# Preparing gate and up inside the attentions, and four pairs of blocks by two levels in the first pass

## The chip, the cores and the metric

The kernel runs on one core of a Trainium2 chip. The metric is device time in microseconds (us) of one execution. Its engines are TensorE (PE; its weight loads are shown as PEld), VectorE (DVE), ScalarE (ACT), GpSimd (POOL) and SyncE (SP), which here only issues transfers. Each engine works through its own instructions in order and waits on semaphores for the others.

## The reference

One decoder layer in float32 on x of 16 batches x 128 rows x 1024 columns, with a context of the same shape:

```python
x = x + self_attention(layernorm(x))            # one head, width 256; Wqkv, Wo
x = x + linear_cross_attention(layernorm(x), ctx)  # 8 heads x 64
x = x + ffn(layernorm(x))
# ffn: 4-bit weights, w = (nibble - zero) * scale per group of 64
Wg, Wu, Wd = dequantize(gate), dequantize(up), dequantize(down)
h = silu(x @ Wg.T) * (x @ Wu.T)                 # 1024 -> 2752
out = h @ Wd.T                                  # 2752 -> 1024
```

The cross attention takes the softmax of the queries over the 64 channels of a head and of the keys over the positions, forms the 64 x 64 context of each head, multiplies, projects, and normalises each column.

## The kernel before, in words

**The feed-forward products are done by Strassen's scheme in Winograd's form**: seven products of half-size blocks in place of eight. The inter dimension of 2752 is cut into ten blocks of 256 (numbers 0 to 9) and a remainder (RB = 10). The tokens are taken in two passes: batches 8 to 15 first (pass 0), then 0 to 7 (pass 1), since the cross attention works on 8 to 15 first.

*By one level* (`one_block`, L1178): gate and up of one block are 7 products each, in the order GATE. A product (`products`, L1140) is four matmuls of 128 x 128 weights with 512 columns, each of which the trace shows as two instructions. The operands T are half-blocks of the normalised x; the weights of all seven products, sums included, lie ready in DRAM (`wprep`).

*By two levels* (`two_levels`, L1360): a pair of blocks (gate and up of both) is seven outer products in the order DOWN, each of them again seven inner ones: 49 products of four matmuls with 256 columns. The left inner operands `li` are combined by POOL (`inner_left`, L1338), the right ones `ti` by DVE (`Operands.inner_right`), four for each outer product. DVE also adds the banks into U, V and C (`got`), and after outer products 2, 3, 7 and 4 ACT takes Silu and DVE multiplies gate with up into `h` (`finish`). In the program the order around outer product n is, on PE: 6, 2, 5, 4 of n, 1 of n+1, 3 of n, 7 of n+1; the `ti` of n+1 are made while n runs. At the end of each outer product the function `between` is called.

Pass 0 does blocks 0 to 5 by one level, pair 3 (blocks 6 and 7) by two, blocks 8 and 9 by one, and then the remainder (`last_block`). Pass 1 does all five pairs by two levels and keeps most right operands from pair to pair. In pass 0 nothing is kept.

**Preparation** (`prepare`, L205) turns the packed bytes into `wprep`. It is a generator that is advanced step by step between other work. A job is one matrix (g, u or d for down) of one block: two steps of dequantising (two shifts or masks of 128 x 512 integers, a subtraction and a multiplication of 128 x 1024, all on DVE, tiles `pa`) and a step of four combinations (`pc`). A job loads two `raw` tiles and their scales and zeros, and stores seven tiles of 256 KB. The remainder has its own jobs r (one step) and m. There are 33 jobs: 20 of g and u, r, m, and 11 of d. Before the change `early` does the first ten (blocks 0 to 4, EARLY = 5) within the self attention, with stores through POOL's queue, and `rest` does the other 23 in pass 0, d and the others in turn, through SP's queue; `beside` and `between` say after which product a step is taken.

**Order.** DVE, PE and SP instructions of the cross attention and of most of what follows are held in program order (`InOrder`). Instructions without that wrapper are placed by the framework's scheduler by the time at which it reckons them ready; on each engine they then run in that order. PE's instructions of block 0 are free in this sense, so that they fill the end of the cross attention.

**The cross attention** works in ticks (`later`, `tick`): eight per batch, one after each key unit and each query unit. The functions of a query unit are put off by ticks: `weigh` (row sums on DVE, multiplication on POOL, tile `qe`), `turn` (DVE transposes into `kt`, SP stores `kd`), `load` one tick later (SP loads `qs`, which must wait until `kd` has landed). `project_out` multiplies `qs` with the mixed context `m_sb` some ticks later and adds the result to X.

**Memory** is given out as stacks from both ends of the SBUF. A later pool lies where an earlier one was, and its first tiles wait until the old ones were last read. On the left, over the self attention's `a_g`, `a_w` (weights `wqkv_sb`, `wo_sb`, biases), come the cross attention's `b_cx` (8 KB per partition), `b_w` (4), `b_0` (8), `b_ek` (12), `b_as` (4), `b_3` in this order, and over these the feed-forward's `c_w` (weights, 20 KB), `c_t`, `c_h`. `block_loads` brings the x of a pass back from DRAM, in eight loads.

Of the kernel before, what the change touches and what calls it, by code (L numbers as in the profile page):

```python
# [66 lines left out]
def decoder_layer(  # L67
# [95 lines left out]
    def prep_pools(stack, name, c, ahead):  # L163
        for key, bufs in (("a", 3), ("c", c), ("raw", ahead + 1), ("sz", ahead + 1)):
            pools[key] = stack.enter_context(
                tc.tile_pool(name=f"{name}_{key}", bufs=bufs, side="right", reuse_waits="tile")
            )
# [4 lines left out]
    def load_raw(blk, mat, s):  # L172
# [3 lines left out]
        if mat == "d":  # L176
            raw, sz = raw[:w], pools["sz"].tile([P, 2, 512], F32, name="szd")[:w]
            nc.sync.dma_start(raw, dq[ds(start // 2, w), ts(s, 512)])
            for g in range(w // 32):
                row = dsz[start // GROUP + g, ts(s, 1024)].rearrange("(t f) -> t f", t=2)  # L180
                nc.sync.dma_start(sz[ts(g, 32)], row.partition_broadcast(32))
# [13 lines left out]
        for m, off, w in parts:  # L195
            q, szs = matrices[m]
            nc.sync.dma_start(raw[:, :, ds(at, w)], q[:, :, ds(off, w)])
            nc.sync.dma_start(
# [6 lines left out]
    def prepare(jobs, ahead, queue, vector=nc.vector):  # L205
# [3 lines left out]
        loads = deque(load_raw(*u) for u in units[:ahead])  # L209
# [6 lines left out]
        for k, (blk, mat, s) in enumerate(units):  # L216
# [6 lines left out]
            if k + ahead < len(units):  # L223
                loads.append(load_raw(*units[k + ahead]))
# [61 lines left out]
    EARLY = 5  # L286

    def give_half(b, h, oT, wo_d, psum, tensor=nc.tensor, vector=nc.vector):
# [19 lines left out]
    prep_pools(first, "q", 4, 1)  # L308
    early = prepare(
        [(blk, mat) for blk in range(EARLY) for mat in "gu"], 1, nc.gpsimd, InOrder(tc, nc.vector)  # L310
    )
    give_pool = ExitStack()
    ag = give_pool.enter_context(tc.tile_pool(name="a_g", bufs=1, reuse_waits="tile"))
    with (
# [166 lines left out]
        for t in range(NT):  # L481
# [38 lines left out]
            else:  # L520

                for i in range(1, BPT):
                    give((t - 1) * BPT + i - 1, oT)
                    value(i, xnT, v)
                atT = turn_weights(at)
# [76 lines left out]
    bcx = unit_pool("b_cx", 2)  # L602
    bw = unit_pool("b_w", 1)
    b0 = unit_pool("b_0", 2)
    bek = unit_pool("b_ek", 3)
    bas = unit_pool("b_as", 1)
    b3 = unit_pool("b_3", 3)
    bkt = side_pool("b_kt", 3)
# [3 lines left out]
    bqs = side_pool("b_qs", 5)  # L612
    b1 = side_pool("b_1", 1)
    b2 = side_pool("b_2", 2)
    bps = side_pool("b_ps", 3, space=PSUM)

# [15 lines left out]
    if True:  # L632
# [8 lines left out]
        sync.dma_start(wk_sb, xwk)  # L641
        sync.dma_start(wq_sb, xwq)
        sync.dma_start(wv_sb, xwv.rearrange("(r p) s -> p r s", p=P))
        sync.dma_start(xwo_sb, xwo.rearrange("(r p) o -> p r o", p=P))
        sync.dma_start(xbo_sb, xbo)
        sync.dma_start(gs_sb, xg)
# [43 lines left out]
        def load_ctx(b):  # L690
# [236 lines left out]
        for d in range(2):  # L927
            wo_again.append(bqs.tile([P, C], F32, name="wo_again", tag="qs"))
            sync.dma_start(wo_again[d], wo[ts(d, P)])
# [12 lines left out]
        for k, b in enumerate(batches):  # L942
# [13 lines left out]
            if len(ahead) == 2:  # L956
                later(2, lambda n=ahead[1]: ctxs.update({n: load_ctx(n)}))
# [68 lines left out]
    with ExitStack() as gs:  # L1026
# [9 lines left out]
        def attention_done():  # L1036

            nonlocal rest
            if plain:
                raise_flag()  # L1040
            sides.close()
            prep_pools(second, "f", 4, 2)
# [858 lines left out]
```

## Time and profile before

| | |
|---|---|
| runs | 2240.55, 2241.54, 2241.73 us; median 2241.54 |
| profiled execution | 2241.3 us; its span 2239.5 us |
| busy in the span | PE 2204.4, DVE 1482.2, POOL 553.1, ACT 468.9 us |
| self attention | 0 to about 250 us |
| cross attention, a batch every 31.2 us | 250 to about 757 us |
| blocks 0 to 5 by one level (block 0 beside the attention's end) | 762 to 1074 us |
| pair 3 by two levels | 1074 to 1162 us |
| blocks 8 and 9, remainder | 1162 to 1299 us |
| pass 1: five pairs, remainder | 1299 to 1760 us |
| down projection | 1760 us to the end |

In the lines below, a group of instructions has its line, engine, operation, output<-input, shapes and count, then the busy time and the mean of one in ns, then the engine's idle time in front of them and who ended it. A line of waits has the total, how often, and the longest. A line of windows has the stretch, its length, and then the busy time of PE, PEld, DVE, ACT and POOL (each with its count), the clock that PE was granted, the share of the 16 DMA engines that was busy, and GB/s.

### The profile page before, as it was taken

Reading aid. Unit: us, or ns where it says so; the run is one execution under the profiler, and the core shown is the slowest. Engines: PE = TensorE matmul, PEld = TensorE weight load, DVE = VectorE, ACT = ScalarE, POOL = GpSimd, SP = SyncE. Lnnn points to the kernel's source line nnn. Section 1 sums busy time; section 2 is a strip of 40 time slices with the busy share of each in tenths; the row PEclk is TensorE's granted clock in tenths of the full one; section 3 lists DMA queues with packets and bytes.
Section 4 is the critical chain, followed back from the end, with each engine's and each line's share of the span. In section 5 each row is a group of like instructions: output and inputs, shape, how many; then the busy total and the mean of one; then the engine's idle time right before and its main releaser. Section 6 shows DMA issues by size and latency. Waiting matters only on the chain.

```text
span 2239.5 us, 24114 instructions
## 1 busy us (share of the span) xinstructions
PE 2204.4 (98%) x8330; PEld 1517.3 (68%) x8330; DVE 1482.2 (66%) x2055; ACT 468.9 (21%) x651; POOL 553.1 (25%) x543
## 2 busy tenths in 40 slices
PE   8999899999999999999999999999999999999998
PEld 7556555555555544444774488888887688888887
DVE  6997466667667657666796658787787645544462
ACT  2111135454554431111111112121121000000000
POOL 5452044444444400001320044444442000000000
PEclk9999999999999999999999999999999999999999
DMA  6435246666686768887649834454554964333731
GB/s 251 157 130 169 85 132 198 209 205 197 208 258 192 225 182 287 284 267 253 199 166 301 251 100 158 167 197 155 175 198 165 350 211 164 114 125 129 226 118 39
DMA packets 270835, 425.23 MB, mean 190 GB/s; under 512 B 28784, under 2 KB 130544, under 8 KB 270576
## 3 DMA queue, kind: packets, MB, share of 16 engines
q1 hardware_dynamic: 244624, 377.72, 52.5%
q0 software_dynamic: 8064, 27.27, 3.3%
q10 hardware_dynamic: 18016, 18.62, 2.7%
q8 instruction: 68, 1.11, 0.2%
q14 instruction: 63, 0.52, 0.1%
HBM read 265.62 MB, written 157.35 MB: 189 GB/s over the span
## 4 chain that ended last, share of the span: by engine, by line
PE 90%; DVE 6%; issue 2%; DMA 1%; POOL 1%; ACT 0%; SPq 0%; DVEq 0%; POOLq 0%; ACTq 0%
PE po L1780 21%; PE q L63 20%; PE p L63 18%; PE kq L63 9%; PE mm L63 8%; PE kx L63 5%; PE mm L396 4%; PE mm L411 2%; DVE pa L63 2%; PE p L1157 1%; PE mm L292 1%; PE tr L343 1%; DVE ti L63 1%; DMA wo_again<-in_wo 0%; POOL qe L806 0%
## 5 line engine op out<-in xcount | busy, mean ns | idle before, releaser
L63 PE MATMUL p<-b,w 128*128 128x512 f32 x560 | 248.2, 596 | 1.9 <-DVE sg L63 1.9
L63 PE MATMUL q<-ti,li 128*128 128x256 f32 x1008 | 232.2, 379 | 3.5 <-DVE ti L63 2.8
L63 POOL TENSOR_TENSOR li<-w 128x512 f32<-128x512 f32 x84 | 118.1, 1408 | 433.3 <-DMA w<-wu 244.8
L63 PEld LDWEIGHTS q<-ti,li 128*128 128x128 f32 x1008 | 191.0, 190 | 31.3 <-issue 2.8
L63 PEld LDWEIGHTS p<-b,w 128*128 128x128 f32 x560 | 106.9, 191 | 136.4 <-issue 128.8
L1780 PE MATMUL po<-wc,lc 128*128 128x256 f32 x840 | 183.4, 379 | 0.0
L63 PE MATMUL p<-T,w 128*128 128x512 f32 x400 | 177.2, 592 | 0.0
L1780 PEld LDWEIGHTS po<-wc,lc 128*128 128x128 f32 x840 | 159.6, 190 | 21.8
L63 ACT COPY k<-q 128x512 f32<-128x512 f32 x126 | 73.7, 585 | 399.2 <-PE q L63 399.2
L63 PEld LDWEIGHTS p<-T,w 128*128 128x128 f32 x400 | 76.0, 190 | 95.7 <-issue 95.2
L1780 PE MATMUL po<-wq,lq 128*128 128x256 f32 x560 | 126.7, 379 | 0.2 <-issue 0.2
L806 POOL TENSOR_TENSOR qe<-qe,qrec 128x1024 f32<-128x1024 f32 x64 | 122.0, 1906 | 11.5 <-DVE qrec L63 9.3
L63 PEld LDWEIGHTS mm<-qs,m_sb 128*128 128x128 f32 x512 | 97.3, 190 | 40.1 <-issue 26.8
L63 PE MATMUL kq<-wk_sb,cx 128*128 128x512 f32 x256 | 120.4, 592 | 2.5 <-DMA cx<-in_cx 2.5
L63 PE MATMUL kx<-ek,cxt 128*128 128x512 f32 x256 | 121.8, 598 | 0.0
L63 PE MATMUL mm<-qs,m_sb 128*128 128x256 f32 x512 | 120.8, 379 | 0.0
L63 PE MATMUL kq<-wq_sb,xn 128*128 128x512 f32 x256 | 120.3, 593 | 0.0
L1780 PEld LDWEIGHTS po<-wq,lq 128*128 128x128 f32 x560 | 106.0, 190 | 15.8 <-issue 0.8
L63 DVE TENSOR_TENSOR pa<-pa,sz 128x1024 f32<-128x1024 int32 x86 | 112.6, 1309 | 2.5
L396 PE MATMUL mm<-xnT,wqkv_sb 128*128 128x512 f32 (+1 forms) x320 | 112.9, 509 | 0.0
L63 DVE STREAM_TRANSPOSE kt<-qe 128x1024 f32<-128x1024 f32 x64 | 79.5, 1242 | 43.7 <-POOL qe L806 43.5
L727 ACT ACTIVATE ek<-kq 128x1024 f32<-128x1024 f32 x64 | 65.3, 1020 | 147.4 <-PE kq L63 147.4
(201 smaller groups left out, 3595.7 us busy)
## 6 DMA issues: line engine op xcount, KB each, us to landing
w<-wu SPq DMA_DIRECT2D x140, 256.0 KB, 3.6
lq<-h SPq DMA_DIRECT2D x140, 256.0 KB, 4.4
w<-wg SPq DMA_DIRECT2D x138, 256.0 KB, 2.8
kd<-kt SPq DMA_DIRECT2D x64, 512.0 KB, 2.9
qs<-kd SPq DMA_DIRECT2D x256, 128.0 KB, 3.2
h<-hc SPq DMA_DIRECT2D x80, 256.0 KB, 2.8
wq<-wd SPq DMA_DIRECT2D x70, 256.0 KB, 5.3
h<-h SPq DMA_DIRECT2D x60, 256.0 KB, 3.0
```

Of the source, the lines that this page charges most:

```text
L63: return lambda *args, **kw: self._tc.keep_in_program_order(fn(*args, **kw))
L292: tensor.matmul(ps, oT[:, d, ts(b % BPT, S)], wo_d[d][:, ts(h, 512)], start=(d == 0), stop=(d == 1),)
L343: nc.tensor.transpose(tr[:, j, :], xn[:, ts(4 * h + j, P)], ident)
L396: nc.tensor.matmul(ps[:, tokens], wqkv_sb[:, f, c, :], xnT[:, c, tokens], start=(c == 0), stop=(c == CC - 1),)
L411: nc.tensor.matmul(ps, xnT[:, c, ts(i, S)], wqkv_sb[:, 4:6, c, :], start=(c == 0), stop=(c == CC - 1),)
L727: nc.scalar.activation(ek, ps, AF.Exp)
L806: nc.gpsimd.tensor_tensor(qe, qe, rec.unsqueeze(2).to_broadcast(wide), ALU.mult)
L1157: tensor.matmul(ps, wt[:, j, :], T[q][:, :, j], start=(first == q and j == 0), stop=(q in (2, 3, 4) and j == JC - 1), skip_group_check=True,)
L1780: nc.tensor.matmul(bank[:, i, :], l[:, ts(i, S)], w,  start=(start and c == 0 and i % 2 == 0), stop=(stop and c == len(pairs) - 1), skip_g ...
```

## The change

- The 33 jobs stand in one list, `todo`: all g and u, then r and m, then the d. `early` takes the first 11 (to g of block 5), with three more steps in the self attention's last quarter. A new generator `middle` takes the next 12 (the rest of g and u, r, m, and d of block 0) within the cross attention, two steps per batch and three in every third, 35 calls; its loads and stores go through SP's queue in program order. `rest` has the ten d that remain, in pass 0.
- Pass 0 does blocks 0 and 1 by one level and the pairs 1 to 4 by two. `rest` is advanced after outer products 1, 2, 6 and 5 of a pair (before: 1, 6 and 5).
- The pools of `middle` (28 KB) come to the right side; `kt` goes from 3 to 2 buffers, `qs` from 5 to 4. On the left the order is now `b_ek`, `b_as`, `b_cx`, `b_0`, `b_w`, `b_3`.
- The cross attention's first loads (its weights, the first two contexts, `wo_again`) are no longer held in program order.
- The first four weight tiles of the feed-forward are loaded through POOL's queue (before: the first through POOL's, the others through SP's).
- The x of pass 1 is loaded in one go after the pairs; before, its eight loads were spread over blocks 8 and 9 and the remainder. The outer operands that need it move from the remainder's start to its m products.

```diff
-    def prep_pools(stack, name, c, ahead):
-        for key, bufs in (("a", 3), ("c", c), ("raw", ahead + 1), ("sz", ahead + 1)):
+    def prep_pools(stack, name, a, ahead):
+        for key, bufs in (("a", a), ("c", 4), ("raw", ahead + 1), ("sz", ahead + 1)):
...
+    todo = [(blk, mat) for blk in range(RB) for mat in "gu"] + [(RB, "r"), (RB, "m")]
+    todo += [(blk, "d") for blk in range(len(BLOCKS))]
+    EARLY, MIDDLE = 11, 23
...
-    prep_pools(first, "q", 4, 1)
-    early = prepare(
-        [(blk, mat) for blk in range(EARLY) for mat in "gu"], 1, nc.gpsimd, InOrder(tc, nc.vector)
-    )
+    prep_pools(first, "q", 3, 1)
+    early = prepare(todo[:EARLY], 1, nc.gpsimd, InOrder(tc, nc.vector))
...
                     give((t - 1) * BPT + i - 1, oT)
                     value(i, xnT, v)
+                    next(early, None)
...
-    bcx = unit_pool("b_cx", 2)
-    bw = unit_pool("b_w", 1)
-    b0 = unit_pool("b_0", 2)
     bek = unit_pool("b_ek", 3)
     bas = unit_pool("b_as", 1)
+    bcx = unit_pool("b_cx", 2)
+    b0 = unit_pool("b_0", 2)
+    bw = unit_pool("b_w", 1)
     b3 = unit_pool("b_3", 3)
-    bkt = side_pool("b_kt", 3)
+    bkt = side_pool("b_kt", 2)
...
-    bqs = side_pool("b_qs", 5)
+    bqs = side_pool("b_qs", 4)
...
+    prep_pools(sides, "x", 2, 1)
+    middle = prepare(todo[EARLY:MIDDLE], 1, sync, vector, sync)
...
-            sync.dma_start(wo_again[d], wo[ts(d, P)])
+            nc.sync.dma_start(wo_again[d], wo[ts(d, P)])
...
+            for n in (3, 5, 7) if k % 3 == 0 and ahead else (3, 7) if ahead else ():
+                later(n, lambda: next(middle, None))
...
-            rest = prepare(jobs, 2, nc.sync, vector)
+            rest = prepare(todo[MIDDLE:], 2, nc.sync, vector)
...
-        PAIRS = [3]
+        PAIRS = [1, 2, 3, 4]
...
-            load_weights(nc.gpsimd if n == 0 else nc.sync)
+            load_weights(nc.gpsimd)
...
                 elif blk == RB:
-                    steps = n in (0, 2, 4)
+                    steps = n in (0, 1, 2)
                 else:
-                    steps = (1, 1 + (mat == "g" and blk < 3), 1, 0, 1, 0, 0)[n % 7]
+                    steps = (1, 1 + (mat == "g"), 1, 0, 1, 0, 0)[n % 7]
...
-            if pass1 and n % 3 == 0:
-                next(pass1_loads, None)
...
-                for k in {("r", 0): (5,), ("r", 1): (7,), ("m", 6): (6,)}.get((mat, q), ()):
+                for k in {("m", 7): (5,), ("m", 6): (7,), ("m", 2): (6,)}.get((mat, q), ()):
                     outer_operand(T1, k)
...
-                    0, PAIRS, first_operands, lambda q: q in (1, 6, 5) and next(rest, None)
+                    0, PAIRS, first_operands, lambda q: q in (1, 2, 6, 5) and next(rest, None)
...
-                pass1_loads = block_loads(1, pass1)
+                for _ in block_loads(1, pass1):
+                    pass
```

## The prediction

> **What bounds the kernel now.** First the page's engine rows, then the list of what TensorE (PE) waited for, then single stages, since the shares are averages.
>
> ```profile
> PE 2204.4 (98%) x8330; PEld 1517.3 (68%) x8330; DVE 1482.2 (66%) x2055; ACT 468.9 (21%) x651; POOL 553.1 (25%) x543
> ```
>
> PE is busy for 2204.4 of 2239.5 us, so 35 us are idle. The largest waits:
>
> ```profile
> PE tr L343 <- ACT xn L152: 9.4, 1, 9.4
> PE p L1157 <- DMA w<-wg: 4.9, 1, 4.9
> PE q L63 <- DVE ti L63: 3.3, 4, 2.4
> PE mm L63 <- DMA wo_again<-in_wo: 3.1, 1, 3.1
> PE kq L63 <- DMA cx<-in_cx: 2.5, 1, 2.5
> ```
>
> So only fewer PE instructions can bring much, and whatever serves PE must keep up. The table of stages shows how far DVE is from that: one batch of the cross attention, four and a half one-level blocks, and the one pair by two levels in the first pass (from its first DVE sum to its last).
>
> ```profile
> 531.23:562.46 31.23, 31.23 (x109) 17.78 (x108) 21.78 (x28) 15.92 (x20) 13.68 (x16) 1.00 0.65 197
> 853.00:1074.00 221.00, 221.00 (x511) 97.73 (x512) 148.32 (x203) 27.22 (x46) 6.25 (x4) 0.99 0.82 267
> 1081.65:1166.30 84.65, 81.32 (x367) 69.09 (x366) 76.07 (x93) 15.04 (x23) 32.64 (x22) 1.00 0.49 160
> ```
>
> After the span and PE's busy time come PEld, DVE, ACT, POOL, clock, DMA share. In the pair DVE is busy for 76.1 of 84.7 us; this is the only stage of the first pass where PE waits for DVE repeatedly (the 3.3 us above). There POOL also stretches DVE's work:
>
> ```profile
> L63 DVE TENSOR_TENSOR pa<-pa,sz 128x1024 f32<-128x1024 f32 x3 | 6.5, 2174 | 0.1
> L63 DVE TENSOR_TENSOR pa<-pa,sz 128x1024 f32<-128x1024 int32 x3 | 4.6, 1540 | 0.1
> L63 DVE TENSOR_SCALAR pa<-raw 128x512 int32<-128x512 int32 x6 | 3.4, 602 | 0.0
> ```
>
> Three dequantisings cost 14.5 us here, 4.83 each; the same four instructions away from POOL's combinations take 0.76 + 2.48 = 3.24 us (DVE's timeline at 190 us).
>
> **1. PE work removed.** PE's timeline gives 3.435 us per product of a one-level block (8 instructions of 512 columns) and 1.727 us per product of a pair (8 of 256 columns). A block is 14 products, 48.1 us; two blocks 96.2. A pair is 49 products, 84.6 us. Three more pairs remove 3 x 11.6 = 34.8 us of PE time. That is the most the change can take from PE's own list.
>
> **2. Is the pair then still PE's?** Per pair DVE now has 76.1 us. In a row of pairs there come four more right operands for the next pair's first product (24 of them took 20.3 us: 4 x 0.85 = 3.4). The three dequantisings go (-14.5) and four steps of down come: of 16 steps over the pairs 11 are dequantisings at 4.83 and five are combinations, four instructions of 0.69 us, 2.8 to 3.9 with the stretch of 4.83/3.24 or so; at 3.3 that makes 17.4 per pair. Sum 76.1 - 14.5 + 3.4 + 17.4 = 82.4 us. To it belong idle times that do not go when DVE is late: four waits of `h` for ACT's Silu (1.37 + 0.87 + 0.59 + 1.18 = 4.0) and 1.4 of gaps between instructions; the 3.2 us of waits for PE can go. So 87.8 us if DVE is fed perfectly, 91.0 if all 8.6 idle us stay. PE needs 84.6. DVE becomes the bound of this stage. I take 89.5, nearer the upper end, since the steps are crowded on the first four outer products and the one after product 2 is followed at once by two `h` of 1.2 us. Four pairs: 358. Before: six blocks and the pair, 6 x 48.1 + 87.9 = 376.5. Gain 18.5 us, not 34.8. Ends: 85.3 per pair (only the stall between pairs) gives -35; all 57 two-SBUF-source instructions stretched by 1.44 like the dequantisings (57 x 0.69 x 1.44 + 28 x 0.69 + 17.4 + 5.4 = 98.7) gives +18.
>
> A rule weighs against this part. The row: a right operand takes 0.68 us alone and up to 1.75 us beside POOL, whose combination takes 1.40. The Trainium skill (SBUF — State Buffer, "SBUF: two separate sides") says that a DVE instruction with two SBUF inputs and a GpSimd instruction exclude each other for the whole length of whichever began. If every POOL combination held DVE up for its whole length, a pair would cost its unstretched 71 us of DVE plus POOL's 32.6 plus 5.4, some 109, and four of them 60 us more than before. The row of the pair says that about 10 of POOL's 32.6 us hit DVE, so I go by the row.
>
> **3. Twelve jobs into the cross attention.** A job is two dequantisings and four combinations, 2 x 3.24 + 2.7 = 9.1 us, or 12.5 with the two-source part stretched by 1.44. Eleven jobs and one short one over the 15 batches with steps: 6.9 to 9.4 us per batch. DVE's idle per batch is 31.23 - 21.78 = 9.4 us, 5.8 of it in one wait for PE just before `ksum`, so the work fits or just fails to. A step goes ahead of the residual add and, in another tick, ahead of a transposed `kt`; behind it wait `kt`, the store `kd`, the loads `qs` and then PE's output product. The last of a batch's four `kt` ends at 536.9 and its product starts at 554.5; its two transfers take 2.9 and 3.2 us and the issues 2, so some 9.5 us of cover lie there. Without cover a step would cost PE its 3 to 4 us. The nearest row of so full a DVE is the first attention at 60 to 130 us: 65.4 of 70 busy and PE lost 1.0. Over 468 us that is 7. I take +6; ends 0 and what rival 2 says. The smaller buffer counts (`kt` 2, `qs` 4) ask for a tile whose last reader was one tick or more before; I cost them at nothing under the same cover.
>
> SP too gets the jobs. Its rows in a batch:
>
> ```profile
> 536.90 0.34 SPq L63 DMA_DIRECT2D kd<-kt  x1
> 539.54 1.93 SPq L63 DMA_DIRECT2D qs<-kd  x4
> 544.85 0.34 SPq L63 DMA_DIRECT2D kd<-kt  x1
> 547.54 1.73 SPq L63 DMA_DIRECT2D qs<-kd  x4
> ```
>
> After each `kd` it stands some 2.35 us until the store has landed. What it has left, the gaps before each `kd`, is 5.6 + 3.4 + 1.3 + 0.2 = 10.4 us per batch. A job issues 11 transfers, 2 x 0.55 + 2 x 0.33 + 1.38 + 2.35 = 5.5 us, 4.4 per batch. 6 us remain: covered, by 1.5 us per `kd`.
>
> **4. One more job in the first attention.** Three steps (9 us) into 218 to 250 us, where DVE has 16 of 32 us idle. They can push `atT` or `v` by up to one step, 3.2 us, against some 2.5 of cover: 0 to +3, I take +1.
>
> **5. The start of the cross attention.** Waits of 3.1 and 2.5 us, and after them PE at clock 0.76 for 7 us (windows 259:266), 1.7 more. `wo_again` no longer stands at the end of SP's list; but `b_0` now lies over `wo_sb`, read until 248.6, so `wvo` lands at about 253.9 instead of 250.5. Ends -7.4 and +3.4; I take -3.
>
> **6. The end of it.** PE waits 4.9 us for the first gate weights, and runs the next 6.2 us at clock 0.57, 2.7 more. The weight pool of 20 KB lay over `b_cx`, `b_w` and `b_0` (in use to 755.9); now it lies over `a_g`, `b_ek` and `b_as` (to about 751). Against that eight issues of 0.59 us go through POOL's queue, in front of `qe` and the `kt` behind it: 4.7 us. Ends -7.6 and +4.7; I take -5.
>
> **7. Second-pass blocks loaded at once.** Eight loads of 512 KB, some 16 us at 267 GB/s, starting when the pair's tiles come free. The first use is after five products of the last block (17 us), the last-loaded tile's after six (21 us). 0 to +5 if late; I take +1. The down steps in blocks 0 and 1 fill a DVE that has a third idle there (148 of 221 busy): nothing, at worst the 1.9 us that PE already waits for `sg`.
>
> **Sum.** -18.5 + 6 + 1 - 3 - 5 + 1 = -18.5. The profiled execution took 2241.3 us, the median of the runs is 2241.5: 2223 us.
>
> **Rivals.**
> Rival 1, PE stays the bound in the pairs: the steps fall into the 3.2 us of PE waits and the Silu waits overlap. For it: in the second pass five pairs run with one stall of 0.6 us. Against: there DVE had no steps, 198 of 257 us busy. 85.3 per pair and +2 for the attention: -35 + 2 + 1 - 3 - 5 + 1, 2202 us.
> Rival 2, slower: SP's queue takes over in the cross attention. Every `qs` waits behind a `kd`, and the jobs put 0.75 to 1 MB of stores in between; 30 MB over 468 us are 64 GB/s on top of 212, and a DMA share of 0.69 becomes 0.90. It decides from the point where a landing takes 1.5 us longer than 2.35 (one in four, with the context loads about it, already takes 4.1). At 4.75 the excess is 4 x 2.4 + 4.4 - 10.4 = 3.6 us per batch, 54 over 15: 2241.3 - 18.5 - 6 + 54 is about 2271 us.
> Rival 3, DVE is stretched more in the pairs: 94 us each, between 89.5 and 98.7, gain 0.5: 2241 us.
> That the change does not do what it says can be excluded: 35 calls stand for the 34 steps of the twelve jobs and their last stores.
>
> **How the numbers follow.** Forecast 58%, own range 2212 to 2237; rival 1 14%; rival 2 15%; rival 3 13%. About 0.2% (4.5 us) is what a measurement can tell from no change. Faster: 56 + 14 + 6 = 76%. Same: 1 + 4 = 5%. Slower: 15 + 1 + 3 = 19%. The range 2203 to 2250 leaves out most of rival 2 and the lower half of rival 1.
>
> **What would show it.** Right: 196 products of 8 PE instructions on 256 columns in one stretch of about 358 us with DVE above 90% busy, PE's waits there for `ti` summing to 15 to 25 us; cross-attention batches of 31.2 us with DVE near 95% busy. Wrong: batches of 33 us or more with PE waiting for `qs` (rival 2) or for `ksum` and `m_sb` (DVE); pairs of 85 us (rival 1) or of 94 and more (rival 3); new waits for `b` in the last block; a clock below 1 after a wait of several us, which would double that wait's price.

## The result, and the profile after

The changed kernel takes 2293.11 us (median of 4 runs, 2290.82 to 2295.49) against 2241.53 us before on the same chip: ratio 1.0231, 95% interval 1.0213 to 1.0249. The forecast was 2223 us; it is slower, by 51.6 us. The profiled execution took 2292.9 us with a span of 2290.8 us. The page's engine row:

```profile
PE 2200.6 (96%) x8834; PEld 1625.7 (71%) x8834; DVE 1694.3 (74%) x2250; ACT 484.2 (21%) x669; POOL 705.5 (31%) x640
```

and PE's longest waits (total, times, longest):

```profile
PE q L63 <- DVE ti L63: 21.1, 16, 3.4
PE mm L63 <- DVE ksum L63: 16.6, 6, 6.0
PE tr L344 <- ACT xn L152: 9.3, 1, 9.3
PE mm L63 <- DMA qs<-kd: 9.1, 2, 7.3
PE p L63 <- DVE sg L63: 5.6, 1, 5.6
PE p L1160 <- ACT qe L800: 5.3, 1, 5.3
```

PE has less to do, as said, yet its busy time fell by only 3.8 us, and its idle time rose from 35 to 90 us. Borders of the stages are read from PE's timeline: the first product with `ksum` (start of the first mix), the first product of block 0, the first product on 256 columns, and so on.

| stage | before | after | |
|---|---|---|---|
| to the first mix of the cross attention | 292.4 | 293.6 | +1.2 |
| from there to the first product of block 0 | 470.3 | 513.2 | +42.9 |
| blocks 0 and 1 | 119.4 | 126.6 | +7.2 |
| the other eight blocks of pass 0 | 377.5 | 376.9 | -0.6 |
| remainder of pass 0 | 37.8 | 37.8 | 0 |
| pass 1 and down projection | 942.2 | 942.7 | +0.5 |

(Before, the eight blocks are six by one level and a pair, with the remainder behind them.) From the tables of windows, first blocks 0 and 1 before, then blocks 0 and 1 and the four pairs after (stretch, length, busy PE, PEld, DVE, ACT, POOL, clock, DMA share, GB/s):

```profile
762.71:882.10 119.39, 116.84 (x290) 56.53 (x291) 72.52 (x105) 34.53 (x47) 11.90 (x15) 0.96 0.78 246
```
```profile
806.79:933.41 126.62, 117.18 (x290) 56.53 (x291) 77.71 (x108) 34.54 (x47) 19.03 (x19) 0.96 0.79 241
933.41:1310.32 376.91, 352.18 (x1570) 301.73 (x1569) 341.00 (x400) 66.35 (x103) 159.97 (x108) 0.98 0.47 150
```

A pair takes 94.2 us, rival 3's figure, with DVE 85.3 busy in each. The attention holds the rest. Its batches after the change, from mix to mix:

```profile
448.79:480.16 31.37, 31.37 (x109) 17.62 (x108) 30.12 (x37) 16.08 (x20) 14.94 (x16) 1.00 0.88 258
480.16:513.71 33.55, 31.47 (x109) 17.70 (x109) 32.91 (x41) 17.09 (x21) 15.19 (x16) 1.00 0.86 266
513.71:548.27 34.56, 34.56 (x108) 19.84 (x109) 31.32 (x39) 14.72 (x18) 16.21 (x18) 0.90 0.90 271
548.27:579.50 31.23, 31.23 (x109) 17.78 (x108) 28.52 (x35) 15.95 (x20) 13.32 (x15) 1.00 0.74 229
...
678.88:725.71 46.83, 34.00 (x109) 18.83 (x108) 33.01 (x41) 17.10 (x21) 15.47 (x16) 0.93 0.81 266
725.71:760.21 34.50, 34.50 (x109) 20.04 (x110) 32.28 (x38) 14.62 (x18) 17.15 (x16) 0.90 0.78 241
```

A batch needs 31.23 us of PE. Where DVE's work stays under that, nothing is lost (first and fourth line). Where three steps bring DVE to 32.9, PE waits 2.1 us for `ksum`, and the next batch, without any wait, takes 34.56 us at a clock of 0.90. In the batch from 579.50 us DVE has 29.9 us of work but stands 2.1 us for `raw`, and PE waits 2.3 us. Over the 15 batches (500.55 us against 458.11) PE was idle for 25.8 us, and its busy time was 16.6 us longer than before with the same instructions. One batch takes 46.8 us, 12.8 of them idle: 9.1 us of waits for `qs` and 3.7 for `ksum`.

### The profile page after: what moved, and what is told of

It is laid out like the page before. It is cut to its first block, busy times and chain, and to the rows that moved or that the text cites. A ratio compares the mean times of both kernels' runs of the same rounds, so it can differ in the third digit from the quotient of the medians.

```text
span 2290.8 us, 25554 instructions
## 1 busy us (share of the span) xinstructions
PE 2200.6 (96%) x8834; PEld 1625.7 (71%) x8834; DVE 1694.3 (74%) x2250; ACT 484.2 (21%) x669; POOL 705.5 (31%) x640
## 3 DMA queue, kind: packets, MB, share of 16 engines
q1 hardware_dynamic: 242752, 374.31, 51.6%
## 4 chain that ended last, share of the span: by engine, by line
PE 71%; DVE 18%; DMA 5%; issue 4%; SPq 1%; POOL 1%; ACT 1%; DVEq 0%; POOLq 0%; ACTq 0%
PE q L63 25%; PE po L1781 21%; PE mm L63 5%; PE kq L63 5%; PE mm L397 4%; DVE pa L63 3%; PE p L63 3%; DVE ti L63 3%; PE kx L63 3%; DVE C L63 2%; PE mm L412 2%; DVE kt L63 2%; PE p L1160 2%; DVE ksum L63 1%; PE mm L295 1%
## 5 line engine op out<-in xcount | busy, mean ns | idle before, releaser
L63 PE MATMUL q<-ti,li 128*128 128x256 f32 x1512 | 356.3, 385 | 21.8 <-DVE ti L63 19.7
L63 PEld LDWEIGHTS q<-ti,li 128*128 128x128 f32 x1512 | 289.2, 192 | 67.1 <-POOL li L63 20.9
L63 ACT COPY k<-q 128x512 f32<-128x512 f32 x189 | 110.5, 585 | 625.0 <-PE q L63 625.0
L63 POOL TENSOR_TENSOR li<-w 128x512 f32<-128x512 f32 x126 | 183.4, 1457 | 185.6 <-PE q L63 87.4
L63 POOL TENSOR_TENSOR li<-w,li 128x512 f32<-128x512 f32 x63 | 86.2, 1367 | 235.9 <-PE q L63 221.8
L63 PE MATMUL q<-b,w 128*128 128x256 f32 x576 | 136.1, 379 | 0.0
L63 DVE TENSOR_TENSOR C<-q,k 128x512 f32<-128x512 f32 x135 | 92.5, 685 | 42.8 <-PE q L63 40.2
L63 POOL TENSOR_TENSOR li<-li,w 128x512 f32<-128x512 f32 x63 | 85.7, 1361 | 121.3 <-PE q L63 121.0
L63 PE MATMUL q<-ti,w 128*128 128x256 f32 x504 | 119.8, 380 | 1.4 <-DVE ti L63 1.4
L63 PEld LDWEIGHTS q<-b,w 128*128 128x128 f32 x576 | 109.4, 190 | 15.7 <-issue 1.0
```

Source lines behind the costliest of these rows:

```text
L63: return lambda *args, **kw: self._tc.keep_in_program_order(fn(*args, **kw))
```

## Experiments

Attention means, as in the table, from the first mix to the first product of block 0 (470.3 before, 513.2 after). Five programs with the same attention code gave 506 to 513 us there, so a few us between such programs mean nothing; programs with the new order of the pools and no jobs in it gave 465.3 to 465.5.

### Which part costs what

**Pairs undone.**

```diff
-        PAIRS = [1, 2, 3, 4]
+        PAIRS = [3]
```

> The changed kernel with only pair 3 by two levels in the first pass (blocks 0 to 5, 8 and 9 by one level, as before the change); the jobs within the attentions stay. Theory A (the loss lies in the attention's 34 steps, and the pairs give nothing because their down steps eat the gain): the attention stays 44 us longer, the first-pass blocks take what they took before the change, less about 2 us since the one pair holds no steps: 2283 us, or 2294 if blocks 0 and 1 still lose their 11 us. Theory B (three more pairs do bring 15 to 18 us and the whole loss is elsewhere): undoing them costs that much, 2308 to 2311 us.

2286.66 us (ratio 1.020, 1.0183 to 1.0217). From the first product of block 0 to pass 1 it takes 537.5 us; the changed kernel 541.3, the kernel before 534.6. Theory A stands: three more pairs do not gain, they cost some 4 us of pass 0. The one pair, now without a step, takes 88.7 us; before the change, with three steps, 88.9. (Four other programs gave 90.6 for the pair as it was before the change, so 2 us in one pair mean nothing.)

**No jobs in the attention.**

```diff
-    middle = prepare(todo[EARLY:MIDDLE], 1, sync, vector, sync)
+    middle = iter(())
+    for blk, mat in todo[EARLY:MIDDLE]:
+        wprep[blk, mat] = wprep[{"r": 0, "m": 0}.get(mat, (blk + 1) % 5), "g"]
```

> The changed kernel without the twelve jobs of the cross attention: their steps, loads and stores are left out, and the weights concerned are read from other blocks' tiles, so that the sums are those of other weights; buffers (kt 2, qs 4), the order of the pools, the pairs and the ten down jobs stay. Theory A (the steps cause the attention's loss, by DVE or by SP): batches back to 31.2 us, the whole 44 us gone, 2249 us. Theory C (the smaller counts of buffers cost by themselves): batches at 32 us or more remain, 2260 us and above. The pairs should stay at 94 us each in both.

2245.29 us (1.0023, 1.0012 to 1.0033). Every full batch takes 31.2 to 31.3 us, with `kt` 2 and `qs` 4:

```profile
471.31:502.54 31.23, 31.23 (x110) 17.78 (x109) 21.69 (x28) 15.91 (x20) 13.69 (x16) 1.00 0.66 202
```

The attention takes 465.5 us. So the jobs cost 513.2 - 465.5 = 47.7 us (41 to 48 over the five programs), the smaller buffers nothing by themselves, and without jobs the attention is 4.8 us shorter than before, as it is with the order of the pools alone (below). The stage of blocks and pairs is the same 541.3 us as in the changed kernel.

**No steps in the pairs.**

```diff
-                    0, PAIRS, first_operands, lambda q: q in (1, 2, 6, 5) and next(rest, None)
+                    0, PAIRS, first_operands, lambda q: None
...
-            rest = prepare(todo[MIDDLE:], 2, nc.sync, vector)
+            rest = prepare(todo[MIDDLE:-6] + todo[-1:], 2, nc.sync, vector)
+            for blk, mat in todo[-6:-1]:
+                wprep[blk, mat] = wprep[0, "d"]
```

> The changed kernel without any down step in the four pairs of the first pass: five down jobs (blocks 5 to 9) are left out and block 0's down weights are read in their place. Theory A (the down steps, 17 to 20 us of DVE per pair, make the pair DVE's): the pair falls from 94.2 to 85.5 us, PE's waits for ti from 21 us to under 5, the whole 35 us less, 2258 us. Theory D (DVE's sums beside POOL's combinations and the slow clock after each wait hold the pair up even without steps): the pair stays above 89 us, 2273 us or more.

2275.70 us (1.0151, 1.0134 to 1.0168). A pair takes 89.4 us (357.6 for four), so theory D: with only 66 us of DVE work per pair it is still 4.8 us above PE's 84.6. PE's timeline shows one wait for `ti` in each pair, 78 to 80 us into it:

```profile
1017.32 1.97 PE L63 MATMUL q<-ti,li 128*128 128x256 f32 x8 [3.28 <-DVE ti L63]
...
1105.44 3.75 PE L63 MATMUL q<-ti,li 128*128 128x256 f32 x8 [3.28 <-DVE ti L63]
```

The second ran its eight instructions in 3.75 us in place of 1.97: slow clock. From 1004 to 1019 us, in front of the first of them, DVE is busy for 14.6 of 15 us, so the pair is too full for DVE at this one place. By its place the wait follows outer product 7, for which the program gives DVE 11 sums, four right operands and two multiplications of `h`; PE needs 12.1 us for an outer product. (Blocks 0 and 1 took 131.9 us in this run; these 5 us more, with waits for `sg` and `h`, I cannot explain.)

### The attention

**No stores.** The jobs' loads and DVE work stay, their stores are left out.

```diff
             while stores:
-                queue.dma_start(*stores.popleft())
+                st = stores.popleft()
+                if keep:
+                    queue.dma_start(*st)
```

> The changed kernel with the twelve jobs' DVE work and loads in the cross attention, but without their stores (the weights are read from other blocks' tiles): SP loses 79 of some 125 transfers and the DMA engines 20 MB. Theory A1 (DVE's time is what lacks): the batches stay as long, the attention within 8 us of the changed kernel's, 2285 to 2293 us. Theory A2 (SP's list is what lacks: kd late, kt buffers late, qs late): at least 25 of the 44 us go, PE's waits for qs and the 8.5 us wait of DVE for kt vanish, 2265 us or less.

2273.86 us (a single execution); attention 496.0, so 17.2 of the 47.7 us go and 30.5 stay. That lies between the two theories' limits; each is a part. The full batch and its follower are there as before:

```profile
478.25:511.62 33.37, 31.47 (x110) 17.70 (x109) 32.81 (x41) 17.12 (x21) 15.37 (x16) 1.00 0.71 213
511.62:546.19 34.57, 34.57 (x109) 19.74 (x110) 31.52 (x39) 14.79 (x18) 16.22 (x18) 0.90 0.74 223
```

**No DVE work.** The counterpart: the same loads and stores, of constant tiles, no dequantising and no combinations.

```diff
-    middle = prepare(todo[EARLY:MIDDLE], 1, sync, vector, sync)
+    middle = transfers()
```

> The changed kernel with the loads and stores of the twelve jobs at the same points of SP's list, but without their DVE work: constant tiles are stored, so the weights concerned are meaningless. The run without stores left 30 us of the attention's 48 (against no jobs at all). Theory A1 (DVE's time does the damage, the stores only add to it): transfers alone cost less than 10 us, the batches 31.2 to 32 us, 2255 us or less. Theory A2 (SP's list and the DMA engines do it): 20 us or more remain, PE waits for qs, 2263 us or more.

2260.64 us (a single execution); attention 482.4, 16.9 us more than without jobs. Again this is between the theories' limits. 30.5 + 16.9 = 47.4: within the scatter, and with one execution of each, the two causes simply add up. All of the 16.9 falls into batches 13 and 14 (42.0 and 32.5 us) and the wait behind the last; the ten before are exactly 31.2. There SP also reloads the first blocks of x (eight loads `b<-xt` of 512 KB from about 610 to 690 us), and DVE stands for a `kt` buffer whose store is late:

```profile
652.54 1.25 DVE L63 STREAM_TRANSPOSE kt<-xn 128x1024 f32<-128x1024 f32 x1 [5.28 <-DMA kd<-kt]
...
664.04 1.25 DVE L63 STREAM_TRANSPOSE kt<-qe 128x1024 f32<-128x1024 f32 x1 [8.42 <-DMA kd<-kt]
```

**Stores through POOL.**

```diff
-    middle = prepare(todo[EARLY:MIDDLE], 1, sync, vector, sync)
+    middle = prepare(todo[EARLY:MIDDLE], 1, InOrder(tc, nc.gpsimd), vector, sync)
```

> The changed kernel with the stores of the cross attention's jobs issued by POOL in program order in place of SP; loads and DVE work as they are. Transfers alone cost 17 us, nearly all in the batches from 640 us on, where SP also reloads the blocks of x. Theory A2a (what lacks there is room in SP's list, where each transfer waits behind the others): most of that goes, 8 to 15 us less than the changed kernel, 2278 to 2285 us, and DVE's long wait for a kt buffer at 677 us goes. Theory A2b (what lacks is the DMA engines' bandwidth, whose share is 0.81 to 0.94 there): the same transfers take the same room, 2290 us or more, also because POOL, which must wait for DVE's combinations before it issues, is late with qe.

2282.06 us (1.0179, 1.0162 to 1.0196); attention 503.4. That is 9.8 us under the changed kernel's 513.2 but only 2.8 under the lowest of the five equal ones, so between 3 and 10 us. The bad batch still takes 43.5, and in it DVE's wait for a `kt` buffer, which by theory A2a would go, is 6.1 us (8.5 in the changed kernel). So a part of the stores' cost lies in SP's list; whether the rest is the DMA engines' stays open. The Trainium skill (DMA: Bandwidth & Descriptors, "Issuing engines are not separate DMA queues") says that another issuing engine saves only the issuing sequencer's time, as all run on the same 16 DMA engines; a gain of 3 to 10 us, where leaving the stores out gave 17.2, does not contradict it.

**What a wait of PE costs.** Two runs put idle work on DVE into the kernel before the change.

```diff
+            vector.tensor_copy(krec, ks)
+            half = st["sum"][:, 1]
+            for _ in range({2: 3, 4: 5, 6: 7, 8: 9, 10: 11}.get(mixes.popleft(), 0)):
+                vector.tensor_tensor(half, half, half, ALU.max)
             vector.tensor_copy(ksum, ks)
```

> The kernel before the change with idle maxima of 128x512 on DVE (0.69 us each) put in front of ksum in five batches of the cross attention: 3, 5, 7, 9 and 11 of them in batches 2, 4, 6, 8 and 10. It measures what one wait of PE costs. Theory E (a wait of PE costs more than itself, since the clock granted afterwards is lower for a time): batches with an idle time of 2 us and more are followed by PE at a clock of about 0.9 for a batch, 1 to 3 us more; the sum over the five batches is clearly above PE's idle time in them. Rival: the low clock of the changed kernel comes from its denser work on the other engines, and here each batch is longer by just the idle time.

2246.31 us (a single execution), and inconclusive: up to 7.95 us more at this point (the eleven maxima of batch 10) made PE wait nowhere in batches 2 to 10 (31.2 to 31.4 us each). So DVE may be several us late there without cost. One wait came two batches later, 2.3 us for `qs` after SP's last reload of x; that batch took 35.5 us, 1.9 more than its work and the wait. The next run delays the last sum, a little before this point.

```diff
                     t = st["sum"]
+                    for _ in range({2: 13, 4: 16, 6: 19, 8: 22}.get(sums_made.popleft(), 0)):
+                        vector.tensor_tensor(t[:, 1], t[:, 1], t[:, 1], ALU.max)
```

> The kernel before the change with 13, 16, 19 and 22 idle maxima of 128x512 on DVE (0.69 us each, 9 to 15 us) in front of the last sum of a key's sums in four batches, so that PE has to wait for it there by some 1 to 7 us. Theory E: after each wait of 2 us and more PE runs at a lower clock, so that a batch with a wait and the one behind it are longer by the wait and 1 to 3.5 us more. Rival: longer by the wait alone, clock 1.00, and the low clock of the changed kernel has another cause (its fuller DVE and DMA).

2268.91 us (a single execution). The two longest waits, each in a batch that ends with it, and the batch behind it:

```profile
444.99:482.81 37.82, 31.39 (x109) 17.62 (x108) 32.58 (x45) 17.12 (x21) 11.40 (x13) 0.98 0.41 121
482.81:516.52 33.71, 33.71 (x109) 19.74 (x110) 23.91 (x31) 14.86 (x18) 16.98 (x19) 0.92 0.76 240
516.52:556.52 40.00, 31.39 (x110) 17.62 (x108) 34.66 (x48) 17.12 (x21) 11.40 (x13) 0.95 0.38 114
556.52:590.91 34.39, 34.39 (x108) 19.96 (x109) 23.39 (x31) 14.61 (x18) 16.98 (x19) 0.91 0.76 237
```

After a wait of 0.83 us the next batch took 31.31 us; after 4.25, 6.43 and 8.61 us it took 33.55, 33.71 and 34.39. Theory E: a wait of some us costs 2.3 to 3.2 us more than itself, with a quiet DVE and a DMA share of 0.76 behind it. The price hardly grows with the wait; in the changed kernel waits of 2.1 and 2.3 us cost 3.3 and 3.2. It is not constant either: in the run with stores by POOL the batches after waits of 1.9 and 2.9 us were 0.6 (0.4 of it another wait) and 1.7 us longer.

**Two steps a batch.** Seven jobs in place of twelve, in batches 1 to 11; three pairs; the step after outer product 2 moved behind 4 (below); buffers `kt` 3 and `qs` 5.

```diff
-    EARLY, MIDDLE = 11, 23
+    EARLY, MIDDLE = 11, 18
...
-            for n in (3, 5, 7) if k % 3 == 0 and ahead else (3, 7) if ahead else ():
+            for n in (3, 7) if 1 <= k <= 11 else ():
...
-        PAIRS = [1, 2, 3, 4]
+        PAIRS = [2, 3, 4]
```

> Seven jobs in the cross attention in place of twelve, two steps in each of batches 1 to 11 and none in the first and the last four, kt 3 and qs 5 as before the change (the down job with its larger scales is no longer there); blocks 0 to 3 by one level, pairs 2 to 4 by two, steps after outer products 1, 6, 5 and 4; the other jobs follow in the first pass. Theory A (an attention batch is lost only where its DVE work passes 31.2 us): attention within 3 us of that without jobs, start of it 1.7 us later than before the change and end 4.8 us earlier; three pairs at 89.4 in place of four blocks and the pair, 280 - 268 = -12; blocks 0 and 1 +3: 2241 + 3 + 2 - 5 - 12 + 3 = about 2232 us. Theory A' (every step costs in proportion, 48 us for 34): 22 steps cost 31 us, about 2260 us.

2252.07 us (1.0041, 1.0029 to 1.0054). Neither figure. The attention takes 480.1 us, 14.6 more than without jobs. Batches 4 to 11 are at 31.2 to 31.3, so two steps a batch are free, as theory A has it. But the first with steps and the one behind it take 32.8 and 33.0 us (DVE stands 6.2 us for the first `raw`, whose load is issued with the step itself), and where SP reloads x there is again a batch of 40.4, with no step in it, behind one of 33.0: SP's list has the last jobs' stores at 644 and 661 us, between the reloads. And PE stands 8.4 us for the flag's sum (`within`, which DVE makes once the attention is done) at the end of block 0.

**Four jobs in batches 2 to 8.**

```diff
-    EARLY, MIDDLE = 11, 18
+    EARLY, MIDDLE = 11, 15
...
-            for n in (3, 7) if 1 <= k <= 11 else ():
+            for n in (3, 7) if 2 <= k <= 8 else ():
...
-                    steps = (1, 1 + (mat == "g"), 1, 0, 1, 0, 0)[n % 7]
+                    steps = (1, 1 + (mat == "g"), 1, 0, 1, 0, int(blk > 1))[n % 7]
```

> As the run with two steps a batch, but only four jobs in the cross attention, in batches 2 to 8, before the blocks of x are reloaded; the other jobs go to blocks 1 to 3, with one step more for each matrix of blocks 2 and 3. Theory (steps cost nothing in a batch that DVE can hold, unless SP also has the blocks of x to reload): the 9.2 and 1.8 us of batches 12 and 11 and the 3.4 us of batches 1 and 2 go, against 2252 us: 2237 us, 2232 if PE's 8.4 us wait for the flag's sum also goes. Rival: the displaced steps make blocks 2 and 3 DVE's or the DMA engines' and give the gain back: 2245 to 2252 us.

2255.73 us (1.0066, 1.0049 to 1.0083), above both figures. The attention takes 471.7 us: the reload of x is undisturbed, the first load still costs 6.2 us (a 2.7 us wait and the slow batch behind it). From 960 to 1000 us the DMA engines are full, with 325 GB/s:

```profile
q1 hardware_dynamic: 6652, 12.99, 103.3%
```

Yet the four one-level blocks, two of them with eleven steps in place of nine, take 222.8 us, against 222.1 in the run before, so the rival does not hold there. The three pairs take 3.2 us more, and the second pass with the down projection 953.7 us in place of 942.3. That is the loss: the last job was left over, DVE does it from 1302.6 to 1314.7 us, POOL stands 11.9 us for DVE's `pa` with a left operand of the second pass, and PE for POOL:

```profile
1312.58 3.78 PE L63 MATMUL q<-ti,li 128*128 128x256 f32 x8 [7.83 <-POOL li L63]
```

What the run would take with all steps in the first pass is not shown.

**Six jobs, kept clear.** Two steps in batches 1 to 9, the first loads issued in batch 0, the flag's sum made right after the last output product.

```diff
-    EARLY, MIDDLE = 11, 18
+    EARLY, MIDDLE = 11, 17
...
         loads = deque(load_raw(*u, sync) for u in units[:ahead])
+        if sync is not nc.sync:
+            yield
...
-            for n in (3, 7) if 1 <= k <= 11 else ():
+            for n in {0: (6,), 10: (3,)}.get(k, (3, 7) if 1 <= k <= 9 else ()):
...
             project_out(b, qs, keys[b], when)
+            if plain and not ahead:
+                later(when[3], raise_flag)
```

> As the run with two steps a batch (seven jobs, three pairs), but six jobs in batches 1 to 9, clear of the reload of x; the first loads of these jobs are issued within batch 0, so that the first step finds its data; the flag's sum is made before the last batch's last row work, where PE need not wait for it. Theory: of 2252 us go 11 (batches 11 and 12), 3.4 (batches 1 and 2) and 8 to 10 (flag): 2229 us, 0.5% below the kernel before. Rival: what is removed at one wait returns at the next, as DVE and SP are full all the same: 2240 us or more.

2242.07 us (1.0001, 0.9992 to 1.0010), not 2229. In the attention the theory holds: 466.2 us, 0.7 more than with no job, at DVE 29.7 of 31.23 and a DMA share of 0.85:

```profile
534.35:565.58 31.23, 31.23 (x110) 17.78 (x108) 29.69 (x37) 15.92 (x20) 14.94 (x16) 1.00 0.85 274
```

The flag's wait, though, has become one of 8.8 us for `h` at the same place.

### The pairs

**The step after product 2 moved behind 4.**

```diff
-                    0, PAIRS, first_operands, lambda q: q in (1, 2, 6, 5) and next(rest, None)
+                    0, PAIRS, first_operands, lambda q: q in (1, 6, 5, 4) and next(rest, None)
```

> The changed kernel with the fourth down step of a pair taken after outer product 4 instead of after 2. Theory D1 (single outer products are over-full for DVE: a step taken after 2 falls into product 6, which already has two multiplications of h; one taken after 4 falls into product 1, which has the fewest sums): the pair falls from 94.2 to about 89.4 us as without steps, 2293 - 19 = 2274 us. Theory D2 (DVE's total of a pair is what counts, 85 of 94 us busy): the pair stays at 93 to 94 us, 2289 to 2293 us.

2281.85 us (1.0173, 1.0156 to 1.0190); a pair takes 91.6 us, from 94.2. The same DVE work at another place gives half of what the steps cost. Theory D1 in its direction, with 2.2 us left above a pair without steps.

```profile
1026.70:1118.30 91.60, 86.64 (x389) 74.18 (x388) 85.62 (x101) 16.47 (x26) 42.37 (x28) 0.98 0.46 152
```

DVE is busy for 85.6 of 91.6 us here, so a total of 85 was not the limit at 94.2.

**U on POOL.** In addition, three sums of outer product 7 go to POOL.

```diff
                 if q == 7:
-                    add_to(U[:, k], U[:, k], m[:, k], ALU.add)
+                    later_u = InOrder(tc, nc.gpsimd).tensor_tensor if ps == 0 else add_to
+                    later_u(U[:, k], U[:, k], m[:, k], ALU.add)
```

> As the run with the step after outer product 4, and in the first pass the three additions to U of outer product 7 (SBUF operands alone) go from DVE to POOL. Theory D1: product 7 is the other over-full one (11 sums, 4 right operands, two multiplications, 13.5 us of DVE in 12.1); without the three sums the wait of 3.3 us at the end of each pair goes, and with it the slow clock behind it: 86 us per pair, 13 us less than the run before. Rival: POOL, 36 of 89 us busy and in order, is late with the left operands or holds DVE up for as long as the three sums took: nothing gained or some us lost.

2297.99 us (1.0246, 1.0229 to 1.0263); a pair takes 95.2 us. The rival, and the groups in the pairs say how: by the program the next sum overwrites the C that POOL still has to read, and DVE waits 15.2 us for POOL there, 3.8 in each of the four pairs.

```profile
L63 DVE TENSOR_TENSOR C<-C,V 128x512 f32<-128x512 f32 x23 | 25.8, 1124 | 15.6 <-POOL U L63 15.2
```

### The end of the attention

**Two pairs, no jobs in the attention.** As the run with four jobs, but:

```diff
-    EARLY, MIDDLE = 11, 15
+    EARLY, MIDDLE = 11, 11
...
-        PAIRS = [2, 3, 4]
+        PAIRS = [3, 4]
```

> No jobs in the cross attention at all; blocks 0 to 5 by one level, pairs 3 and 4 by two, all jobs after the eleventh in blocks 0 to 5 and the two pairs (after outer products 1, 6, 5, 4); order of the pools, the first attention and the loads as in the change. From the runs: end of the attention -4.8, its start +1.7, blocks 8 and 9 (96.2 us) become a pair of 91 us, -5, blocks 0 and 1 +3: 2236 us. If displaced steps make blocks 2 to 5 wait for DVE or DMA: 2241 us and more.

2256.35 us (1.0068, 1.0052 to 1.0085). Blocks 0 to 5 take 329.5 us in place of 311.8: 8.4 us for the flag's sum at the end of block 0, and 8.6 us for `h` before the pairs.

**Order of the pools and POOL's loads alone**, in the kernel before the change.

```diff
-    bcx = unit_pool("b_cx", 2)
-    bw = unit_pool("b_w", 1)
-    b0 = unit_pool("b_0", 2)
     bek = unit_pool("b_ek", 3)
     bas = unit_pool("b_as", 1)
+    bcx = unit_pool("b_cx", 2)
+    b0 = unit_pool("b_0", 2)
+    bw = unit_pool("b_w", 1)
...
-            load_weights(nc.gpsimd if n == 0 else nc.sync)
+            load_weights(nc.gpsimd)
```

> The kernel before the change with two of its parts alone: the order of the pools on the left, and the first four weight tiles loaded through POOL's queue. The prediction's step 6 as it stood: PE's wait of 4.9 us for the first gate weights goes, with the 2.7 us of slow clock behind it; the run without jobs in the attention showed the end 4.8 us earlier but a start 1.7 us later: 2237 to 2239 us. Rival: the time freed there only lets PE run ahead into block 0 and is lost again at the wait for sg or for the flag's sum: 2241 us.

2245.93 us (1.0021, 1.0012 to 1.0030): the rival. PE starts block 0 at 758.7 in place of 762.7 us and then loses it:

```profile
812.02 1.89 PE L63 MATMUL mm<-qs,m_sb 128*128 128x256 f32 x8
813.75 1.02 PE L1157 MATMUL p<-T,w 128*128 128x512 f32 x2
815.26 1.12 PE L63 MATMUL mm<-sq,ones 128*128 128x512 f32 x2 [0.50 <-ACT sq L869]
816.23 3.60 PE L1157 MATMUL p<-T,w 128*128 128x512 f32 x8
828.19 0.58 PE L63 MATMUL mm<-within,ones 128*128 128x1 f32 x2 [8.37 <-DVE within L63]
```

Between the last batch's output products PE's list now has more of block 0 than before, so that the last row sums (`mm<-sq`) start at 815.3 us in place of 810.3, and behind them one product is left that needs nothing of DVE, where there were three. All that DVE does for the last batch, in program order, comes later too, and PE waits for it.

**Order of the pools alone**, the weights loaded as before the change.

```diff
-            load_weights(nc.gpsimd)
+            load_weights(nc.gpsimd if n == 0 else nc.sync)
```

> The kernel before the change with the order of the pools on the left alone; the first weight tiles are loaded as before the change (one through POOL, three through SP), and PE's list at the end of the attention is the one of before. Theory F (the two parts of step 6 do opposite things: the order of the pools ends the wait for the first weights; POOL's loads let the scheduler put too many products of block 0 ahead of the last batch's row sums, which then hold DVE and PE up for 8.4 us): the 4.9 us wait and its slow clock go, no 8.4 us wait, 2235 to 2238 us. Rival: the time is lost at the end of block 0 all the same, 2241 to 2246 us.

2233.47 us (0.9968, 0.9957 to 0.9980): 0.3% under the kernel before. Theory F holds. PE's first products of block 0 and the row sums at the end:

```profile
756.79 3.60 PE L1157 MATMUL p<-b,w 128*128 128x512 f32 x8
...
802.03 1.02 PE L63 MATMUL mm<-sq,ones 128*128 128x512 f32 x2
802.88 1.02 PE L1157 MATMUL p<-b,w 128*128 128x512 f32 x2
803.74 3.60 PE L1157 MATMUL p<-T,w 128*128 128x512 f32 x8
807.18 3.60 PE L1157 MATMUL p<-b,w 128*128 128x512 f32 x8
810.61 3.60 PE L1157 MATMUL p<-T,w 128*128 128x512 f32 x8
814.86 0.38 PE L63 MATMUL mm<-within,ones 128*128 128x1 f32 x2 [0.66 <-DVE within L63]
```

No wait, so no slow clock either: the first eight instructions take 3.60 us, before the change 6.44.

**The mended version with the weights by SP.** The same line undone in the run with six jobs.

```diff
-            load_weights(nc.gpsimd)
+            load_weights(nc.gpsimd if n == 0 else nc.sync)
```

> As the mended version (2242 us), with the first weight tiles loaded as before the change. Theory F: the 8.8 us wait for h at the end of block 0 and 2 us of slow clock behind it go: 2231 us, 0.4 to 0.5% below the kernel before. Rival: the wait comes back at another place of block 0 or 1: 2238 us or more.

2233.83 us (0.9968, 0.9959 to 0.9977). The 8.8 us wait is gone; the three pairs (91.3 us each) and the 18 steps of the attention just pay for themselves, as the order of the pools alone gives the same time.

## Why the prediction was wrong

**Step 3, "I take +6", failed most.** It measured +47.7 against no jobs. Two errors. The sum was one of means: 29.6 us of DVE work in a batch of 31.23 fits, and the run with 18 evenly placed steps, clear of the reload of x, shows that it costs 0.7 us; but three dequantisings and combinations in one batch (32.9 us) do not fit, nor do three steps in the 20.9 us before the second mix (PE stands 6.0 us there, once). And the cover for SP was read in a batch where SP has nothing else to load; it does not hold while the blocks of x return, where DVE stood 8.5 us for the second `kt` buffer. That the smaller buffer counts cost nothing is right without jobs. Beside them no run changes the counts alone; DVE does wait for a `kt` buffer in that stretch, but with three buffers a batch of 40.4 us remained.

**The price of a wait was missing from the sum.** I put the slow clock into the last sentence as a sign, and into steps 5 and 6, but not into steps 2 and 3. In the attention it is 16.6 of 42.9 us.

**Step 2, "I take 89.5" for a pair,** measured 94.2. DVE's work was close (85.3 against 82.4), its idle time at the upper end (9.0 against 5.4 to 8.6). But the reasoning failed, since it added DVE's work over the whole pair: 89.4 is what a pair takes with no step at all, as the stretch of outer product 7 is too full for DVE by itself, and DVE's waits for PE, 3.2 us that "can go", are 5.7 us in each pair. The step after product 2 then costs 2.6 us more than the same step after product 4. The 109 us weighed there, for POOL's combinations holding DVE up throughout, did not come; the rule itself (the Trainium skill, SBUF — State Buffer, "SBUF: two separate sides") no run here tests.

**Step 1** holds: PE's list is shorter by what was said. Since a pair written like this takes 89.4 by itself, the most that three of them can bring is 3 x (96.2 - 89.4) = 20 us, not 34.8.

**Step 6, "-5", was right on the order of the pools and wrong on the loads.** The order alone gives 8 us: 4.8 in the attention and 1.1 at its start, and behind it 2.4 net (2.8 of slow clock in the first eight instructions of block 0), near the end of -7.6. POOL's loads were priced by their issue time in front of `qe` (and PE does wait 5.3 us for `qe`); in the kernel before the change they also alter PE's order and cost 12 us (2245.9 against 2233.5). In the changed kernel PE's order stayed nearer to the old one (2.4 us for `within`).

**Step 5, "-3",** measured with step 4 +1.2: the two waits stayed at 3.1 and 2.5 us, now for `wvo` and `wo_again` (before for `wo_again` and `cx`). The fourteen programs with the eleventh early job reach the first mix at 293.0 to 296.8 us (mean 294.4), the five with ten, whatever the order of the pools, at 291.3 to 293.5 (292.3): steps 4 and 5 together cost about 2. No run separates them.

**Step 7's "nothing" for blocks 0 and 1** cost 7.2 us: PE's wait for `sg` grows from 1.9 to 5.6 us, that for `within` from 0.6 to 2.4, and one of 1.5 for `h` is new. By the trace DVE waits there for `szd` and for the stores of earlier `pa`: only down jobs are left for these blocks, whose scales come in four transfers per step. No run tests this. The loads of x cost nothing, as far as the last block shows.

**The rivals.** Rival 2 named the place and nearly the size (+48 in the attention), but SP and its transfers are about a third of it, DVE two thirds, so that its size was luck in part. Rival 3's pair was right to 0.2 us. I gave them 28% together and as alternatives; both came true at once, rival 2 in part.

## What to carry to other kernels

Whether added work fits is decided in the fullest interval between two points where the critical engine depends on it, not in the mean of a stage; spread it so that no interval passes its length, and issue its first load an interval ahead. Price each wait of PE of about 2 us and more with its slow clock as well, 2 to 3 us here. When a transfer is moved to another queue, compare the order of the critical engine's list before and after: the scheduler may fill the gap with work that pushes a chain behind it.

## What the runs showed of the hardware

A single wait of 1.9 to 8.6 us costs PE 0.2 to 3.3 us more in the batch behind it (six of the eight such waits read here 2.3 or more), and one of 0.83 us nothing. In windows of 2 us from the end of the 2.1 us wait at 513.71 us in the changed kernel, the granted clock is 0.57, 0.50, 0.50, 0.73 and then 1.00: about 7 us near half speed. It does not come each time: the same wait of 2.4 us for `ti` in the one pair is followed by eight instructions in 1.97 us, without slow clock, in the kernel before the change (pair 88.9 us), and in 2.58 us with the order of the pools alone (pair 90.6). The Trainium skill (TensorE: Matmul & The Clock Gate, "Part 1: The HAM clock gate") says that the clock goes to half after an idle window of about 3.4 us and back after as long a busy one. By that figure one slow window would cost some 1.7 us (an estimate from the page). The half speed agrees; but waits shorter than that window, 2.1, 2.3 and 2.7 us, already cost over 3 us.
